# A four-layer graph kernel on one core: SAGE's gathered rows taken apart into a float32r leading part and an exact rest

## The chip, the core and the metric

The kernel runs on one core of a Trainium2 chip (trn2). Times are microseconds of device time of that core. The time before the change is 3072.85 us, the median of three runs (3069.26 to 3073.18). One more execution was profiled; it took 3070.05 us, and its span, from the first to the last instruction, is 3067.8 us.

## The reference

The model has 3327 nodes with 512 features, padded to 3328 = 26 blocks of 128, and a sparse 0/1 adjacency matrix. Each of four layers normalizes the rows, takes the positive part, runs a graph layer and adds its result to the rows. Layers 0, 2 and 3 are attention layers. Layer 1, which the change touches, is GraphSAGE:

```python
mask = (adj > 0).astype(x.dtype)
deg = jnp.sum(mask, axis=1, keepdims=True)
agg = mask @ x / jnp.maximum(deg, 1.0)
self_f = x @ W_self + b_self
nb_f = agg @ W_nb + b_nb
combined = jnp.concatenate([self_f, nb_f], axis=-1)
out = combined @ W_comb + b_comb
return jax.nn.relu(out)
```

Everything is float32. `mask @ x` is what the changed lines compute: for each node the sum of its neighbours' rows.

## The kernel before, in words

**Lists.** The kernel doesn't multiply by the whole mask. The nodes that receive are cut into 52 groups of 64 (`GB`), two to a block of 128 (`PG` = 2, counted by `u`). For each group a first stage lists the nodes that any of its 64 members has as a neighbour, in *chunks* of 128. How many chunks a group may have stands in `CAPS`: 22, 15, 13, 12, 11, 10, 9 and so on down to 5 and 4, in all 359. A chunk's 128 rows are fetched with one indirect DMA (`gather`, issued on GpSimd's queue at L995); a mask of 128 x 64 bytes (`mask`) says which of its rows belongs to which of the group's 64 nodes.

**Stages.** `sparse` runs attention layer 0 (`attend`), then the batch norm and layer norm of its result, then SAGE, then attention layers 2 and 3. While SAGE ends a block, `Following` (`proj`) already prepares the table of layer 2 from it: norm, transposes, three products, and two stores.

**SAGE.** The normalized rows are stored to `h_dram` (L1266). `own` multiplies each block by the weights for the node itself (`s_ps`, L1276) and adds the bias (L1277). Then come the *parts*: a part takes up to two chunks (`SUNIT`) of each of a block's two groups. For a part, `load` takes per group a tile `z_rows` (one of 8 buffers, `SROWS`), casts the byte mask to float32 with ScalarE into `z_mask` (L1333), and gathers the rows. The main loop asks for part i + 2 (`SAHEAD`) and then multiplies part i: one float32 matmul per chunk, mask as the stationary side (128 x 64), rows as the moving side (128 x 512), into the 64 partitions of `sage_acc` that belong to group `u` (L1352). The two groups of a block alternate, chunk by chunk.

When a block's sums are there, `ending` divides them by the degree on ScalarE (`s_ag`, L1291), transposes them with TensorE (`a_ps`, L1295), copies them (`aT`, L1297), multiplies by the neighbour weights (`n_ps`, L1301), and on VectorE adds the own part and the residual (`s_o`, L1306 and L1307). `Following.norm` and `rest` go on: three ScalarE passes over `s_o`, a few small VectorE operations (`rs_h`, `rs_g`, `rs_y`, L633 to L639), `ln_h` (L694), transposes (`p_ps`, L701), products (`p_sd`, L708 and L710; `p_wh`, L722), the small rows `v_row` and `r_row` (L713, L716, L719), and eight scalings of `p_wh` into `v_row` (L730). These steps are generators; `tick()`, called once per row of chunks, moves each by one step.

**What sets the order.** The attention layers' order is written out by hand. The SAGE stage isn't: a scheduler places its instructions on each engine's queue when the program is built, so that, for example, the matmuls of a part stand among those of `ending` and `Following`. Each engine then works through its own queue in order and waits at semaphores. A buffer is free for its next use when the last reader is done: a gather into `z_rows` waits for the matmuls of the part four parts earlier.

Of the kernel before, what the change touches and what calls it, by code (L numbers as in the profile page):

```python
# [22 lines left out]

F32 = mybir.dt.float32
BF16 = mybir.dt.bfloat16
I32 = mybir.dt.int32
I8 = mybir.dt.int8
U8 = mybir.dt.uint8
# [2 lines left out]
ALU = mybir.AluOpType  # L31
# [5 lines left out]
P = 128  # L37
H = 8
F = 64
D = H * F  # L40
# [8 lines left out]
GB = 64  # L49
CAPS = (22, 15, 13, 12, 11, 10, 9, 9, 9) + 4 * (8,) + 6 * (7,) + 11 * (6,) + 21 * (5,) + (4,)  # L50
# [5 lines left out]
UNIT = 3  # L56
SUNIT = 2
SROWS = 8
SAHEAD = 2
SMALL = 53.0  # L60
SHIFT = 20.0
# [4 lines left out]
def general(ctx: ExitStack, tc: tile.TileContext, t: dict, out: bass.AP):  # L66
# [22 lines left out]
    x3 = dram.tile([NP, D], F32, name="x3")  # L89
    bias_dram = dram.tile([NP, NP], BF16, name="bias_dram")  # L90
    recip_dram = dram.tile([1, NP], F32, name="recip_dram")
# [4 lines left out]
    nc.vector.memset(ones, 1.0)  # L96
    ones_bf = const.tile([P, P], BF16, name="ones_bf")
    nc.vector.memset(ones_bf, 1.0)
# [6 lines left out]
    with tc.tile_pool(name="setup", bufs=2) as sp, tc.tile_pool(name="setup1", bufs=1) as s1, tc.tile_pool(  # L105
# [4 lines left out]
        for c in range(NB):  # L110
            a = sp.tile([P, NP], I32, name="adjT_i", tag="adjT_i")
            nc.sync.dma_start(a, t["adjT"][c * P : (c + 1) * P, :])
            m = sp.tile([P, NP], BF16, name="mask_bf", tag="mask_bf")
            nc.vector.tensor_scalar(m, a, 0.0, None, ALU.is_gt)
# [7 lines left out]
        for b in range(nbk):  # L122
            w = min(BANK, NP - b * BANK)
            nc.vector.tensor_copy(deg[:, b * BANK : b * BANK + w], deg_ps[:, b, :w])
        alone = s1.tile([P, NP], BF16, name="alone")
        nc.vector.tensor_scalar(alone, deg, 0.0, -OFF, ALU.is_equal, ALU.mult)
# [25 lines left out]
    def gat(layer, xin, W, a_i, a_j, finish):  # L152

        with ExitStack() as lx:
# [58 lines left out]
            with tc.tile_pool(name=f"mx{layer}", bufs=2) as mp, tc.tile_pool(  # L213
# [3 lines left out]
                for q in range(NQ):  # L217
# [6 lines left out]
                    for c in range(NB):  # L224
                        mb = mp.tile([P, QW], BF16, name="mb", tag="mb", bufs=3)
                        if layer == 0:
                            a = mp.tile([P, QW], I32, name="adj_i", tag="adj_i", bufs=2)
                            nc.sync.dma_start(a, t["adj"][c * P : (c + 1) * P, q0 : q0 + QW])
# [4 lines left out]
                        for h in range(H):  # L233
                            junk = mp.tile([P, QW], BF16, name="junk", tag="junk", bufs=2)
                            nc.vector.tensor_tensor_reduce(
# [218 lines left out]
def products(ctx, tc, t):  # L454
# [5 lines left out]
    WA = pool.tile([P, 3, KC, 2 * H], F32, name="WA")  # L460
    ok = pool.tile([1, 1], I32, name="ok")
    with tc.tile_pool(name="wa1", bufs=1) as wp, tc.tile_pool(name="wa_ps", bufs=1, space=PSUM) as wps:
# [67 lines left out]
def constants(ctx, tc, N):  # L530
# [19 lines left out]
    c["pow"] = pw = const.tile([P, WB], F32, name="fpow")  # L550
    pi = const.tile([P, WB], I32, name="fpow_i")
    nc.gpsimd.iota(pi, pattern=[[-1, WB]], base=0, channel_multiplier=1)
# [10 lines left out]
class Projection:  # L563
# [4 lines left out]
    last, pb = "wh_ps", 1  # L568
# [10 lines left out]
    def block(self, c):  # L579
# [22 lines left out]
        for h in range(H):  # L602
            nc.scalar.mul(V[:, h, 0:F], wh[:, h * F : (h + 1) * F], V[:, h, F : F + 1])
        nc.sync.dma_start(self.table[c * P : (c + 1) * P, :ROW], row.bitcast(I32))

# [39 lines left out]
class Following:  # L645
# [29 lines left out]
    last = "p_ps"  # L675
# [291 lines left out]
def sparse(ctx: ExitStack, tc: tile.TileContext, t: dict, out: bass.AP, WA, ls, cs, idx, rdeg, first):  # L967
# [5 lines left out]
    nc = tc.nc  # L973
# [4 lines left out]
    PG = P // GB  # L978
# [13 lines left out]
    mask = keep.tile([P, NCH, GB], U8, name="mask")  # L992
# [167 lines left out]
    with ExitStack() as mx:  # L1160
# [64 lines left out]
        gp = mx.enter_context(tc.tile_pool(name="fsage", bufs=2))  # L1225
        gps = mx.enter_context(tc.tile_pool(name="fsage_ps", bufs=2, space=PSUM))
        two = [P, 2, D]
        with tc.tile_pool(name="fbn", bufs=1) as bp:
            var_ps = gps.tile([P, D], F32, name="var_ps", tag="n_ps")
            for c in range(0, NB, 2):  # L1230
# [3 lines left out]
                for i in range(2):  # L1234
                    k = used(c + i)
# [7 lines left out]
        with tc.tile_pool(name="fln", bufs=1) as bp:  # L1243
# [40 lines left out]
            for i in range(2):  # L1284
                own(NB - 2 + i)

        ends = []

        def ending(b, acc):
# [21 lines left out]
        def tick():  # L1311
            for e in list(ends):
                if next(e, 0) == 0:
                    ends.remove(e)
            proj.tick()


        parts = []
# [3 lines left out]
        loaded = {}  # L1322

        def load(i):
            if i >= len(parts):
                return
            zs = loaded[i] = []
            for u, kn in enumerate(parts[i][1]):
                if kn is not None:
                    k0, n = kn  # L1330
                    zt = gp.tile([P, SUNIT, D], F32, name="z_rows", tag="z_rows", bufs=SROWS)
                    mf = gp.tile([P, SUNIT, GB], F32, name="z_mask", tag="z_mask", bufs=SROWS)
                    nc.scalar.copy(mf[:, :n, :], mask[:, k0 : k0 + n, :])  # L1333
                    for k in range(n):
                        gather(zt[:, k, :], h_dram, k0 + k)
                        zs.append((k, u, k0 + k, mf[:, k, :], zt[:, k, :]))
            zs.sort(key=lambda x: x[:2])

        for i in range(SAHEAD):
            load(i)  # L1340
        for i, (b, _, begins, stops) in enumerate(parts):
            load(i + SAHEAD)
            if begins:
                acc = gps.tile([P, D], F32, name="sage_acc", tag="sage_acc")
            at = -1
            for r, u, k, m, z in loaded.pop(i):
                if r != at:
                    at = r
                    tick()
                g = b * PG + u  # L1350
                f, l = k == ls.first[g], k == ls.first[g] + CAPS[g] - 1
                nc.tensor.matmul(acc[u * GB : (u + 1) * GB, :], m, z, start=f, stop=l)  # L1352
            if stops:
                ends.append(ending(b, acc))
        while ends:
# [95 lines left out]
```

## Time and profile before

| what | value |
|---|---|
| time, median of 3 | 3072.85 us |
| profiled execution | 3070.05 us |
| its span | 3067.8 us |
| busy: PE, PEld, DVE, ACT, POOL | 2324.5, 1434.3, 1781.0, 1162.7, 1375.4 us |
| mean granted TensorE clock | 0.788 |
| first and last gather of `z_rows` | 1107.9 and 1704.6 us |
| first and last `s_ag` (block 0, block 25) | 1200.3 and 1727.8 us |
| `sage_acc` matmuls: records, busy | 718, 210.6 us |
| `z_rows` gathers: count, busy, mean | 359, 341.2 us, 950 ns |

How to read the profile: the engines are PE (TensorE), PEld (its weight loads, which overlap PE), DVE (VectorE), ACT (ScalarE), POOL (GpSimd) and SP. A row of a group names the line, the engine, the operation, out<-in by the program's names, shapes, how often; then busy us and mean ns, then the idle time just ahead of these instructions and what ended it. The matmuls' ends are modelled. In the timeline a row begins with the start and the duration in us; xN says how many equal instructions were merged, and brackets show idle time of the engine before it and what ended it. "issue" is time in which an engine waited for nothing that the profile shows. The page's chain of work that ended last is followed back from the last instruction. A few per cent of the matmul records can be missing.

### The profile page before, as it was taken

What the parts mean: (1) busy time and instruction counts of PE and PEld (TensorE: products, weight loads), DVE (VectorE), ACT (ScalarE), POOL (GpSimd) and SP (SyncE); (2) the same over time, 40 slices, a digit from 0 to 9 for tenths busy, and PEclk for the clock granted to TensorE, in tenths of its full rate; (3) what the DMA queues carried; (4) which work ended last, traced back from release to release, by engine and by line L of the source; (5) the groups of instructions that cost most, each with busy time, mean ns of one, the idle gap of its engine ahead of it and who ended that gap; (6) DMA issues with size and microseconds to landing.
All of it is one profiled execution on the core that took longest, in us unless ns stands there. A gap on an engine that the chain in (4) does not pass through costs nothing.

```text
span 3067.8 us, 55727 instructions
## 1 busy us (share of the span) xinstructions
PE 2324.5 (76%) x22046; PEld 1434.3 (47%) x22046; DVE 1781.0 (58%) x2077; ACT 1162.7 (38%) x4117; POOL 1375.4 (45%) x1462
## 2 busy tenths in 40 slices
PE   2888157877777797788888857888998857778876
PEld 1555034555554342333333345555665445555654
DVE  7434867787786840000111077777766457887886
ACT  3775012233334321344444402444666601222343
POOL 0000055566553026666554266555444155665653
PEclk9888678886777898889999867887877766675666
DMA  7671067777664455666666366566655256666774
GB/s 284 242 266 58 11 221 236 218 242 210 201 196 145 168 178 172 192 205 218 192 194 185 105 177 190 177 184 193 183 172 175 72 170 185 187 196 194 200 198 131
DMA packets 186641, 561.55 MB, mean 183 GB/s; under 512 B 35386, under 2 KB 40322, under 8 KB 183045
## 3 DMA queue, kind: packets, MB, share of 16 engines
q0 software_dynamic: 114880, 404.47, 45.2%
q1 hardware_dynamic: 70918, 153.04, 14.2%
q8 instruction: 177, 2.90, 0.4%
q14 instruction: 92, 0.75, 0.1%
q10 hardware_dynamic: 574, 0.39, 0.0%
HBM read 498.42 MB, written 59.36 MB: 182 GB/s over the span
## 4 chain that ended last, share of the span: by engine, by line
PE 63%; issue 13%; ACT 5%; DVE 2%; another core or an unknown queue 2%; DMA 1%; POOL 0%; DVEq 0%; SPq 0%; ACTq 0%; POOLq 0%
PE facc L1117 30%; PE p_wh L722 7%; PE r_bc L1028 6%; PE sage_acc L1352 5%; PE n_ps L1301 3%; PE p_sd L710 2%; PE p_sd L708 2%; PE s_ps L1276 2%; PE fwx_ps L1194 1%; PE bmean_ps L1204 1%; PE p_ps L701 1%; ACT v_row L730 1%; PE a_ps L1295 1%; DMA fWc<-in_L_gnn_W_comb 1%
## 5 line engine op out<-in xcount | busy, mean ns | idle before, releaser
L995 POOL DMA_INDIRECT rows<-table,idx x1077 | 1027.7, 954 | 1222.8 <-PE facc L1117 350.9
L1117 PE MATMUL facc<-rows,wgt 128*64 128x65 f32 x17232 | 958.0, 270 | 371.5 <-issue 358.0
L1117 PEld LDWEIGHTS facc<-rows,wgt 128*64 128x64 f32 x17232 | 820.8, 179 | 668.7 <-issue 588.7
L1103 DVE TENSOR_TENSOR wgt<-mx,mask 128x1536 f32<-128x1536 f32 (+1 forms) x405 | 638.4, 1576 | 168.2 <-PE facc L1117 78.6
L1096 DVE TENSOR_TENSOR mx<-r_bc,rows 128x1536 f32<-128x1536 f32 (+1 forms) x405 | 639.5, 1579 | 161.1 <-PE facc L1117 68.4
L995 POOL DMA_INDIRECT z_rows<-h_dram,idx x359 | 341.2, 950 | 395.2 <-ACT hT L1273 138.8
L1055 ACT ACTIVATE fhp<-sums,rd 64x64 f32<-64x64 f32 x832 | 219.7, 334 | 145.5 <-DVE rd L1049 71.3
L1028 PE MATMUL r_bc<-r_one,fones 1*128 1x512 f32 x312 | 217.8, 783 | 16.6 <-DMA r_one<-r_dram 8.6
L1352 PE MATMUL sage_acc<-z_rows,z_mask 128*64 128x512 f32 x718 | 210.6, 641 | 14.0 <-issue 7.7
L722 PE MATMUL p_wh<-fWt,hT 128*128 128x512 f32 x416 | 214.5, 661 | 2.0 <-ACT r_row L716 1.8
L1088 ACT ACTIVATE mask<-on 128x192 uint8<-128x192 uint16 (+1 forms) x135 | 46.5, 344 | 445.4 <-DVE on L1082 181.8
L1045 ACT COPY sums<-facc 128x260 f32<-128x260 f32 x156 | 57.5, 369 | 407.6 <-PE facc L1117 289.3
L719 DVE TENSOR_SCALAR r_row<-r_row 8x128 f32<-8x128 f32 x52 | 11.7, 226 | 307.3 <-ACT r_row L716 224.0
L1306 DVE TENSOR_TENSOR s_o<-n_ps,bn_y 128x512 f32<-128x512 f32 x26 | 17.9, 688 | 206.9 <-PE n_ps L1301 190.3
L722 PEld LDWEIGHTS p_wh<-fWt,hT 128*128 128x128 f32 x416 | 84.6, 215 | 107.1 <-issue 101.3
L589 PE MATMUL wh_ps<-fWt,hT 128*128 128x512 f32 x208 | 121.3, 709 | 2.8 <-ACT hT L776 2.8
L730 ACT ACTIVATE v_row<-p_wh,v_row 128x64 f32<-128x64 f32 x416 | 89.7, 321 | 73.8 <-PE p_wh L722 72.5
L1055 ACT ACTIVATE bn_y<-sums,rd 64x64 f32<-64x64 f32 x416 | 109.5, 333 | 2.4 <-DVE rd L1049 0.5
L1301 PE MATMUL n_ps<-fWx,aT 128*128 128x512 f32 x208 | 106.1, 649 | 5.1 <-ACT aT L1297 4.9
L1352 PEld LDWEIGHTS sage_acc<-z_rows,z_mask 128*64 128x64 f32 x718 | 51.7, 142 | 119.9 <-issue 105.6
L1276 PE MATMUL s_ps<-fWx,hT 128*128 128x512 f32 x208 | 96.1, 616 | 9.0 <-ACT hT L1273 9.0
L713 ACT ACTIVATE v_row<-p_sd 128x8 f32<-128x8 f32 x52 | 9.6, 184 | 240.5 <-PE p_sd L710 107.3
(196 smaller groups left out, 2291.3 us busy)
## 6 DMA issues: line engine op xcount, KB each, us to landing
adj_i<-in_adj SPq DMA_DIRECT2D x26, 1664.0 KB
table<-v_row SPq DMA_DIRECT2D x78, 264.0 KB
rows<-table,idx POOLq DMA_INDIRECT x1077
fin_x<-fx SPq DMA_DIRECT2D x52, 256.0 KB
ln_x<-in_x SPq DMA_DIRECT2D x26, 256.0 KB
bn_x<-in_x SPq DMA_DIRECT2D x13, 512.0 KB
fx<-bn_x SPq DMA_DIRECT2D x13, 512.0 KB
fsage_x<-fx SPq DMA_DIRECT2D x26, 256.0 KB
```

What stands on the lines that cost most here:

```text
L589: nc.tensor.matmul(wh, hT[:, kc, :], self.Wt[:, kc, :], start=(kc == 0), stop=(kc == KC - 1))
L722: nc.tensor.matmul(wh, hT[:, kc, :], self.Wt[:, kc, :], start=(kc == 0), stop=(kc == KC - 1))
L730: nc.scalar.mul(V[:, h, 0:F], wh[:, h * F : (h + 1) * F], V[:, h, F : F + 1])
L995: nc.gpsimd.indirect_dma_start(out=dst, out_offset=None, in_=src[:, :], in_offset=bass.IndirectOffsetOnAxis(ap=idx[:, k : k + 1], axis=0))
L1028: nc.tensor.matmul(rb, ones[0:1, :], rrs.pop(g), start=True, stop=True)
L1055: nc.scalar.mul(hp[o0 : o0 + GB, h * F : (h + 1) * F], sm[mine, q, 0:F], rd[mine, q, :])
L1096: nc.vector.tensor_tensor(mx[:, :n], rbs[g].unsqueeze(1).to_broadcast(full), gt[:, :n, H * (F + 1) : ROW].unsqueeze(3).to_broadcast(full), ...
L1103: nc.vector.tensor_tensor(wt[:, :n], mx[:, :n], mk.unsqueeze(2).to_broadcast(full), ALU.mult)
L1117: nc.tensor.matmul(accs[g][v * GB : (v + 1) * GB, q * (F + 1) : (q + 1) * (F + 1)], wt[:, k, h, :], gt[:, k, h * (F + 1) : (h + 1) * (F + 1)],
L1276: nc.tensor.matmul(ps, hT[:, kc, :], Wx[:, 0, kc, :], start=(kc == 0), stop=(kc == KC - 1))
L1301: nc.tensor.matmul(ps, aT[:, kc, :], Wx[:, 1, kc, :], start=(kc == 0), stop=(kc == KC - 1))
L1352: nc.tensor.matmul(acc[u * GB : (u + 1) * GB, :], m, z, start=f, stop=l)
```

## The change

In the SAGE stage, each gathered row tile is taken apart on VectorE: `z_high` is the row rounded to float32r, and what is left over replaces the row itself, in place. The masks are now float32r as well, and as wide as the block: 128 columns, of which the 64 of the other group stay zero, in eight tiles that are cleared once. Each chunk becomes two float32r matmuls, of the high and of the low part, into all 128 partitions of `sage_acc`; both groups of a block sum into the same accumulation, with one start and one stop per block. `halves(i + 1)`, the splitting of the next part, is asked for ahead of the matmuls of part i. `z_high` has four buffers (`SHALF`), `z_rows` still eight. The changed lines, with the imports and constants:

```diff
+F32R = mybir.dt.float32r
+SHALF = 4
@@ SAGE
+        hp = mx.enter_context(tc.tile_pool(name="fhalf", bufs=1))
...
                     zt = gp.tile([P, SUNIT, D], F32, name="z_rows", tag="z_rows", bufs=SROWS)
-                    mf = gp.tile([P, SUNIT, GB], F32, name="z_mask", tag="z_mask", bufs=SROWS)
-                    nc.scalar.copy(mf[:, :n, :], mask[:, k0 : k0 + n, :])
+                    mf = wide[u][i % len(wide[u])]
+                    nc.scalar.copy(mf[:, :n, u * GB : (u + 1) * GB], mask[:, k0 : k0 + n, :])
                     for k in range(n):
                         gather(zt[:, k, :], h_dram, k0 + k)
-                        zs.append((k, u, k0 + k, mf[:, k, :], zt[:, k, :]))
-            zs.sort(key=lambda x: x[:2])
+                    zs.append((u, k0, n, mf, zt))
+
+        def halves(i):
+            if i >= len(parts):
+                return
+            zs = []
+            for u, k0, n, mf, zt in loaded.pop(i):
+                zh = hp.tile([P, SUNIT, D], F32R, name="z_high", tag="z_high", bufs=SHALF)
+                nc.vector.tensor_copy(zh[:, :n, :], zt[:, :n, :])
+                zl = zt.bitcast(F32R)
+                nc.vector.tensor_tensor(zl[:, :n, :], zt[:, :n, :], zh[:, :n, :].bitcast(F32), ALU.subtract)
+                zs += [(k, u, k0 + k, mf[:, k, :], zh[:, k, :], zl[:, k, :]) for k in range(n)]
+            split[i] = sorted(zs, key=lambda x: x[:2])
+
+        split = {}
+
+        wide = []
+        for u in range(PG):
+            wide.append([])
+            for i in range(SAHEAD + 2):
+                mf = gp.tile([P, SUNIT, P], F32R, name=f"z_mask{u}{i}", bufs=1)
+                nc.vector.memset(mf.bitcast(F32), 0.0)
+                wide[u].append(mf)
         for i in range(SAHEAD):
             load(i)
+        halves(0)
         for i, (b, _, begins, stops) in enumerate(parts):
             load(i + SAHEAD)
+            halves(i + 1)
             if begins:
                 acc = gps.tile([P, D], F32, name="sage_acc", tag="sage_acc")
-            at = -1
-            for r, u, k, m, z in loaded.pop(i):
-                if r != at:
-                    at = r
-                    tick()
-                g = b * PG + u
-                f, l = k == ls.first[g], k == ls.first[g] + CAPS[g] - 1
-                nc.tensor.matmul(acc[u * GB : (u + 1) * GB, :], m, z, start=f, stop=l)
+            zs = split.pop(i)
+            for r in sorted({z[0] for z in zs}):
+                tick()
+                for half in (4, 5):
+                    for z in zs:
+                        if z[0] == r:
+                            last = stops and half == 5 and z is zs[-1]
+                            nc.tensor.matmul(acc, z[3], z[half], start=begins, stop=last)
+                            begins = False
             if stops:
                 ends.append(ending(b, acc))
```

## The prediction

> **What bounds the kernel now.** I read the page first, then the windows of the SAGE stage, the timeline, the waits and the chain inside those windows, and last the built order of both programs. Only the SAGE stage changes: the gathers from `h_dram` run from 1108 to 1705 us, its last `s_ag` is at 1727.8. I split it at 1160 (the last `own`) and at 1447 (the `s_ag` of block 10; the 26 blocks count from 0). The stretches below give us of busy time and (records) of PE, PEld, DVE, ACT, POOL, then granted clock, DMA share, GB/s; a second answer gives the same for `sage_acc` alone.
>
> ```profile
> 1108.00:1160.00 52.00, 46.36 (x132) 20.47 (x132) 6.92 (x10) 5.22 (x13) 20.69 (x22) 0.93 0.38 112
> 1160.00:1447.00 287.00, 223.23 (x764) 86.28 (x760) 20.96 (x57) 93.87 (x389) 182.67 (x192) 0.89 0.65 198
> 1447.00:1730.00 283.00, 248.16 (x923) 109.80 (x924) 33.25 (x92) 136.84 (x562) 137.74 (x146) 0.92 0.58 180
> ```
>
> ```profile
> 1160.00:1447.00 287.00, 116.93 (x392) 30.48 (x388) 7.15 (x11) 0.89 0.65 198
> 1447.00:1730.00 283.00, 88.16 (x308) 19.97 (x308) 11.08 (x16) 0.92 0.58 180
> ```
>
> The late stretch (15 blocks of 9 to 12 chunks, a chunk being one gather of 128 rows) is TensorE's: 248 of 283 us. In the heavy stretch a gather costs POOL 0.95 us and 0.30 us of issue, so 192 x 1.25 = 240 of 287 us: POOL and PE (223) share the bound. DVE has next to nothing to do. In the chain, `sage_acc` has 27.7% of the heavy stretch and 22.3% of the late one.
>
> The timeline of PE says what a chunk costs now:
>
> ```profile
> 1512.34 1.07 PE L1352 MATMUL sage_acc<-z_rows,z_mask 128*64 128x512 f32 x2
> 1519.17 3.60 PE L722 MATMUL p_wh<-fWt,hT 128*128 128x512 f32 x8
> 1522.70 3.65 PE L1352 MATMUL sage_acc<-z_rows,z_mask 128*64 128x512 f32 x16
> 1526.87 1.08 PE L1352 MATMUL sage_acc<-z_rows,z_mask 128*64 128x512 f32 x4
> ```
>
> An f32 matmul is two records. A full-width one takes 0.43 us a record (x8 in 3.60), 0.86 a matmul. A chunk alone takes 1.07, but two chunks (x4) also 1.08, and eight (x16) 3.65: a pair for groups u=0 and u=1, which write the two halves of PSUM's partitions, runs side by side.
>
> **What the Trainium skill says.** "FP8 and Floating Point Precision", TensorE Precision Notes: true FP32 is four passes of the array, the reduced form a truncation to some 22 bits. Four passes in 0.86 us fit; a pass of 512 columns is then 0.215 us (estimate); no f32r runs here yet. "TensorEngine Tiling (Array Packing)", When to Use Tiling: a stationary side of 64 columns or fewer allows two column tiles at once. The x2 and x4 rows agree. "VectorE: DVE Perf Modes", the perf-mode tier table: an fp32 copy in SBUF reaches 2x, `tensor_tensor` stays at 1x. `L897` and `L853` below agree. "SBUF — State Buffer", SBUF: two separate sides: while DVE runs a 2-port op (an fp32 copy is one), GpSimd can't write a gather's descriptors until that op ends. The trace shows it even for an op with two SBUF inputs:
>
> ```profile
> 1237.59 0.94 POOL L995 DMA_INDIRECT z_rows<-h_dram,idx  x1 [0.30 <-issue]
> 1237.96 0.69 DVE L1306 TENSOR_TENSOR s_o<-n_ps,bn_y 128x512 f32<-128x512 f32 x1 [11.36 <-PE n_ps L1301]
> 1238.68 0.69 DVE L1307 SCALAR_TENSOR_TENSOR s_o<-s_o,fsage_x 128x512 f32<-128x512 f32 x1
> 1238.84 1.35 POOL L995 DMA_INDIRECT z_rows<-h_dram,idx  x1 [0.30 <-issue]
> ```
>
> The gather that starts inside L1307 ends 0.82 us after it and takes 1.35 instead of 0.94. One that is under way when L1306 starts (an input in PSUM) takes 0.94. A DVE op already started isn't lengthened.
>
> **The change, part by part.**
>
> *Matmuls.* 359 chunks were 718 records; they become 718 f32r matmuls (each row of gathers: high, low) of 128 columns, all into the whole of PSUM's partitions, so nothing is paired. At one pass: 718 x 0.215 = 154 us against 210.6 busy (116.9 + 88.2 + 5.5). But a pair goes from 4 x 0.215 = 0.86 side by side to 4 x 0.215 in a row: nothing is won there. What is won is chunks alone: the timeline has 26 lone x2 groups, each 1.07 to some 0.58 (two passes and the same 0.15 of start): 13 us; the rest of the 57 us is half-clock time after stalls, which stays. I take -10 us of path; bounds -35 (all of it counts where PE is the bound) to +50 (f32r needs two passes, or its weight loads don't hide; the `p_sd` rows, x8 in 0.95 us, put a weight load at 0.12 us at most, under a pass of 0.215).
>
> *DVE splits.* Per group and part one copy and one subtraction; the mask casts count 163 of two rows and 33 of one. Prices:
>
> ```profile
> L853 DVE TENSOR_SCALAR adj_b<-adj_i 128x3328 bf16<-128x3328 int32 x26 | 49.0, 1885 | 8.4 <-DMA adj_i<-in_adj 6.4 <-PE words_ps L859 2.0
> L1232 DVE TENSOR_TENSOR bn_d<-bn_y,bn_mean 128x1024 f32<-128x1024 f32 x13 | 15.8, 1225 | 14.0 <-PE var_ps L1236 8.5 <-ACT bn_d L1233 5.5
> L897 DVE TENSOR_SCALAR bit<-at 116x1664 int32<-116x1664 int32 x11 | 11.3, 1024 | 0.3
> ```
>
> L853 and L897 (one SBUF input, one with a cast) give (1885 - 1024) / 1664 = 0.52 ns an element: a copy of 1024 is 0.69 us, of 512 0.43; at 1x it would be 1.23, the upper bound. Subtractions: 1.23 (L1232) and 0.69. Sum: 163 x 1.92 + 33 x 1.12 = 350 us on an engine that was busy 54 of 570 us. A full part (4 chunks) is 4 x 0.06 of gaps + 3.83 = 4.07 us of DVE.
>
> *POOL against DVE.* With DVE busy 4.07 us of a part of about 6 (0.68), a gather starting at random waits 0.68 x the mean rest of an op (sum of squares 3.97 / 2 x 3.83 = 0.52) = 0.35 us. Cadence 1.60, times 192 = 307 us against 287: +20 in the heavy stretch. If gathers fall into step with the op ends, 1.3 us, 250 us, hidden: 0. Late: 10 x 1.6 = 16 of 18.6 us a block, hidden.
>
> *DVE's queue.* It is in order, and holds `s_o`, `r_row`, `rs_h`, `rs_g`, `rs_y` of the next layer's rows. Their waits were free:
>
> ```profile
> DVE r_row L719 <- ACT r_row L716: 185.9, 19, 21.0
> DVE s_o L1306 <- PE n_ps L1301: 181.3, 17, 48.4
> ```
>
> In the built order after, a late block's DVE queue is: six copies and six subtractions, then `s_o` to `rs_y`, then the next block's. From `s_o` to the end of `rs_y` the trace has 5.2 us (1607.45 to 1612.68) and, every second block, where ScalarE comes late, 10.5 us (1622.28 to 1632.78). The splits of ten chunks are 9.9 us and 12 gaps, 10.6. In a row: 15.8 and 21.1, mean 18.5 us. Now such blocks take 19.9 and 17.3 us between their `s_ag`s, mean 18.6. So DVE's row becomes as long as TensorE's cycle, no longer; two queues of one length that wait for each other lose something, of which I take +5 us for the 15 blocks. Behind the waiting `r_row` stand the copies, behind them TensorE's matmuls, behind those the buffers that POOL waits for (8, still). Bounds: 0 if ScalarE comes in time, +40 if all blocks take DVE's 21.1 (2.5 us in each of 15).
>
> *Start.* In the built order all `s_ps` now precede the first `sage_acc`; before, seven chunks ran among them and six more gathers (22 by 1160, against the 16 that eight buffers hold) were issued: 6 x 1.25 = 7.5 us, I take +5; bounds 0 and +8. Memsets of eight masks: in DVE's free 3 us between `bn_d`s, 0; the same number of mask casts, 0.
>
> Sum: -10 + 20 + 5 + 5 = +20 us. Profiled execution: 3067.8 of span, 3070.05 in all, so 3090; the shown median is 2.8 above it: 3093.
>
> **Rivals.** *DVE hides everything, faster: this is the one on the other side.* DVE stood idle nine tenths of the stage, PE is the largest share of the chain. Late sage work falls from 88 to 154 chunks x 0.43 = 66 us, -22; heavy -10: 3073 - 32 = 3041. Against it: the DVE row of 18.5 us a late block. It comes about if ScalarE is no longer late in every second block. *f32r not in one pass:* a matmul of 0.43 us makes 309 us of them; late PE is 248 / 15 = 16.5 us a block now and 16.5 + (132 - 88) / 15 = 19.5 then, at today's share of 0.88 22.1 against 18.7, +51; with heavy +40 (of 200 x (0.86 - 0.58) = 56 and POOL's 20 together) 3073 + 91 = 3164. A loss that I count as small becomes a plain one from some 0.3 us a matmul on. Against: the skill's four passes. *GpSimd shut out* of the 0.06 us gaps between splits, so gathers and splits alternate: 4.07 + 5.0 = 9.1 us a part in place of 6, 192 x 2.27 = 436 against 287, +149: 3222 or more. It decides once a gather loses two gaps in a row. Nothing in the trace shows two such ops in a row with a gather waiting. *No change:* gains and losses cancel, within 6 us.
>
> **How the numbers follow.** My forecast 0.43 (own range 3079 to 3130), faster 0.26, no change 0.14, two passes 0.10, GpSimd shut out 0.07. A measurement tells about 0.2%, 6 us. Faster 0.26, same 0.14, slower 0.43 + 0.10 + 0.07 = 0.60. The range leaves out the shut-out case and the outer edges of faster and two passes: 3040 to 3160.
>
> **What would show it.** Right: `sage_acc` busy near 160 to 175 us at some 0.22 us a matmul; DVE 350 us more; z_rows gathers with a mean of 1.2 to 1.4 us; `z_high` copies behind waits for ACT `r_row`; the last `s_ag` at 1740 to 1760. Wrong: gathers still 0.95 us; late blocks 16 to 17 us apart (faster); 0.43 us per f32r matmul (two passes); gathers of 2 us (shut out).

## The result, and the profile after

The changed kernel takes 3072.66 us (median of 12 runs), the kernel before beside it 3073.86 us (12 runs): ratio 1.0003, 95% interval 0.9986 to 1.002. That is no change that can be measured; 20 us more were forecast. The profiled execution of the changed kernel has a span of 3077.7 us, 9.9 more than that of before; 8.7 of them lie ahead of the first gather of the SAGE stage, in work that is the same in both.

One thing has to be said before any number is compared: every kernel of this case ran in one of two kinds of session. In some, to which the times above belong, the kernel before takes 3025 to 3081 us (**B sessions** below), in others 2615 to 2633 us (**A sessions**). The forecast was made from a trace of a B session. All ratios are taken within one session. The expectations quoted below speak of "kinds of chips"; but the same chip number showed both kinds, so what differs is not known to be the chip.

The stage in the three stretches of the prediction, cut at the same events: *start* from the first gather to the `s_ag` of block 0, *heavy* to that of block 10, *late* to that of block 25.

| profiled execution, us | start | heavy | late | stage |
|---|---|---|---|---|
| before, on record | 92.4 | 246.4 | 281.1 | 619.9 |
| changed, on record | 102.7 | 262.8 | 255.8 | 621.3 |

So the change moves much: +10, +16 and -25 us. The same windows as shown for before, first of all instructions, then of `sage_acc` alone (us of busy time and records of PE, PEld, DVE, ACT, POOL; then clock, DMA share, GB/s):

```profile
1116.60:1219.00 102.40, 72.45 (x187) 36.90 (x185) 41.77 (x51) 9.63 (x27) 55.04 (x43) 0.83 0.37 107
1219.00:1482.00 263.00, 212.63 (x704) 127.47 (x703) 168.61 (x233) 93.58 (x376) 205.48 (x170) 0.86 0.64 197
1482.00:1738.00 256.00, 237.48 (x917) 146.90 (x916) 171.70 (x269) 136.00 (x552) 179.53 (x148) 0.95 0.65 198
```

```profile
1116.60:1219.00 102.40, 32.03 (x75) 18.01 (x75) 0.00 (x0) 0.83 0.37 107
1219.00:1482.00 263.00, 119.51 (x332) 68.79 (x331) 6.90 (x10) 0.86 0.64 197
1482.00:1738.00 256.00, 96.41 (x313) 59.52 (x312) 10.84 (x16) 0.95 0.65 198
```

The busy time of `sage_acc` has not fallen: it is 248 us in all, 210.6 before. That column misleads here: it is made of the modelled lengths of single matmuls, for an f32r matmul 0.4 us or more (0.475 on average). What a matmul costs in the row is read from the starts. The timeline of PE:

```profile
1587.58 0.63 PE L1381 MATMUL sage_acc<-z_rows,z_mask 128*128 128x512 f32 x2
1588.05 0.62 PE L1381 MATMUL sage_acc<-z_high,z_mask 128*128 128x512 f32 x2
1588.51 0.62 PE L1381 MATMUL sage_acc<-z_rows,z_mask 128*128 128x512 f32 x2
1588.97 0.62 PE L1381 MATMUL sage_acc<-z_high,z_mask 128*128 128x512 f32 x2
```

Two matmuls every 0.465 us: 0.23 each, one pass. In the stretches where the granted clock is 0.5, most start 0.43 apart. The groups on the page:

```profile
L998 POOL DMA_INDIRECT z_rows<-h_dram,idx x359 | 440.1, 1226 | 307.3 <-ACT hT L1276 140.6
...
L1353 DVE TENSOR_TENSOR z_rows<-z_rows,z_high 128x1024 fp32r<-128x1024 f32 (+1 forms) x196 | 214.0, 1124 | 0.3
...
L1351 DVE CAST z_high<-z_rows 128x1024 fp32r<-128x1024 f32 (+1 forms) x196 | 126.3, 662 | 124.6 <-DMA z_rows<-h_dram,idx 82.4
```

The splits cost 214.0 + 126.3 = 340 us of DVE. A gather has gone from 0.95 to 1.226 us. In the heavy stretch POOL has 205.48 us of gathers and 170 x 0.30 of issue, 256 of 263 us: **GpSimd is its bound now**. And the waits of DVE in the late stretch, where `r_row` had waited for ScalarE before:

```profile
DVE rs_h L636 <- ACT ln_j L688: 20.9, 10, 2.5
DVE z_high L1351 <- DMA z_rows<-h_dram,idx: 13.5, 7, 4.8
DVE s_o L1310 <- PE n_ps L1305: 10.3, 5, 3.5
...
DVE r_row L722 <- issue: 3.6, 1, 3.6
```

Of the waits for `r_row`, 66.4 us behind ScalarE in the late stretch of before, 5 us are left. Where it came from is seen in a block of the late stretch of before, in the timeline:

```profile
1622.97 1.04 PE L710 MATMUL p_sd<-hT,WA 128*8 128x128 f32 x8
...
1624.95 3.70 PE L722 MATMUL p_wh<-fWt,hT 128*128 128x512 f32 x8
...
1629.41 0.19 ACT L713 ACTIVATE v_row<-p_sd 128x8 f32<-128x8 f32 x1 [10.19 <-PE p_wh L722]
...
1629.90 0.28 DVE L719 TENSOR_SCALAR r_row<-r_row 8x128 f32<-8x128 f32 x1 [6.20 <-ACT r_row L716]
```

and in one of the changed kernel:

```profile
1602.47 1.04 PE L713 MATMUL p_sd<-hT,WA 128*8 128x128 f32 x8
...
1603.55 0.18 ACT L716 ACTIVATE v_row<-p_sd 128x8 f32<-128x8 f32 x1 [5.13 <-PE p_sd L713]
```

`v_row` needs `p_sd`. In before, ScalarE stood idle for 5.4 us after the recorded end of `p_sd` (1624.01) until it could start; in the changed kernel 0.04 us. (The ends of matmul records are modelled, but `p_wh`, behind it in the queue, has its start at 1624.95.) I call this a **late hand-over**: TensorE's result reaches the others later than its records say. Counted for this one place (from the recorded end of `p_sd` to `v_row`, as far as ScalarE was idle, for the 24 that come before the last `s_ag`): before has 17 of 24 later than 1 us, 93.7 us in all, 41.1 of them in the late stretch; the changed kernel 3, 9.6 and 1.4.

Two other explanations can be looked for in the trace of before. `v_row` might have waited for the store of an older `v_row` tile; but in all 17 cases the semaphore that TensorE steps, and that `v_row` waits for, makes its last step 0.02 us before `v_row` starts (here it stands still from 1622.26 to 1629.38). TensorE might have run at half clock, more slowly than its records show; but in only 3 of the 17 cases does the granted clock fall below 1.0 between the recorded end of `p_sd` and `v_row` (here it is 1.0 from 1604.2 to 1634.9). So it is TensorE's signal that comes late, and in most cases not for a lower clock. Whether TensorE itself worked later than its records say isn't shown.

### The profile page after: what moved, and what is told of

It is laid out like the page before. It is cut to its first block, busy times and chain, and to the rows that moved or that the text cites. A ratio compares the mean times of both kernels' runs of the same rounds, so it can differ in the third digit from the quotient of the medians.

```text
span 3077.7 us, 56471 instructions
## 1 busy us (share of the span) xinstructions
PE 2330.7 (76%) x22046; PEld 1529.4 (50%) x22046; DVE 2103.2 (68%) x2477; ACT 1168.4 (38%) x4117; POOL 1472.8 (48%) x1462
## 4 chain that ended last, share of the span: by engine, by line
PE 58%; issue 16%; ACT 4%; DVE 4%; DMA 2%; POOL 1%; another core or an unknown queue 0%; DVEq 0%; SPq 0%; ACTq 0%; POOLq 0%
PE facc L1120 29%; PE r_bc L1031 6%; PE p_wh L725 6%; PE sage_acc L1381 4%; PE n_ps L1305 3%; PE p_sd L713 2%; PE p_sd L711 2%; DMA z_rows<-h_dram,idx 1%; PE fwx_ps L1197 1%; PE s_ps L1279 1%; PE bmean_ps L1207 1%; POOL z_rows L998 1%; PE p_ps L704 1%; DVE z_rows L1353 1%; ACT fhp L1058 1%
## 5 line engine op out<-in xcount | busy, mean ns | idle before, releaser
L1120 PE MATMUL facc<-rows,wgt 128*64 128x65 f32 x17232 | 946.6, 269 | 379.9 <-issue 351.5
L998 POOL DMA_INDIRECT z_rows<-h_dram,idx x359 | 440.1, 1226 | 307.3 <-ACT hT L1276 140.6
L1353 DVE TENSOR_TENSOR z_rows<-z_rows,z_high 128x1024 fp32r<-128x1024 f32 (+1 forms) x196 | 214.0, 1124 | 0.3
L1351 DVE CAST z_high<-z_rows 128x1024 fp32r<-128x1024 f32 (+1 forms) x196 | 126.3, 662 | 124.6 <-DMA z_rows<-h_dram,idx 82.4
L1381 PE MATMUL sage_acc<-z_high,z_mask 128*128 128x512 f32 x359 | 148.0, 479 | 49.6 <-DVE z_high L1351 30.1
L1381 PE MATMUL sage_acc<-z_rows,z_mask 128*128 128x512 f32 x359 | 148.5, 472 | 24.3 <-DVE z_rows L1353 16.9
L1381 PEld LDWEIGHTS sage_acc<-z_high,z_mask 128*128 128x128 f32 x359 | 74.5, 210 | 90.2 <-issue 54.9
L707 ACT ACTIVATE hT<-p_ps 128x128 f32<-128x128 f32 x208 | 55.6, 283 | 137.5 <-PE facc L1120 89.1
```

Source lines behind the costliest of these rows:

```text
L998: nc.gpsimd.indirect_dma_start(out=dst, out_offset=None, in_=src[:, :], in_offset=bass.IndirectOffsetOnAxis(ap=idx[:, k : k + 1], axis=0))
L1120: nc.tensor.matmul(accs[g][v * GB : (v + 1) * GB, q * (F + 1) : (q + 1) * (F + 1)], wt[:, k, h, :], gt[:, k, h * (F + 1) : (h + 1) * (F + 1)],
L1351: nc.vector.tensor_copy(zh[:, :n, :], zt[:, :n, :])
L1353: nc.vector.tensor_tensor(zl[:, :n, :], zt[:, :n, :], zh[:, :n, :].bitcast(F32), ALU.subtract)
L1381: nc.tensor.matmul(acc, z[3], z[half], start=begins, stop=last)
```

## The experiments

All stages, by the cuts above; the ratio is that of the times, to the kernel before in the same session, with its interval. Each row of stretches is one profiled execution. e1, e2 and e3 (A) and e7 (B) are the kernels of e9, e16, e10 and e13 once more. Two traces of one kernel differ in a stretch by up to 9 us in A (hybrid, late: 243.3 and 234.2) and 15 us in B (dead bn_stats, heavy: 278.5 and 293.4), so that smaller differences between two rows say little.

| kernel | session | start, heavy, late | stage | ratio of times |
|---|---|---|---|---|
| before (e11) | A | 66.4, 214.2, 230.1 | 510.7 | |
| changed (e12) | A | 94.9, 257.5, 240.5 | 592.8 | 1.0289 (1.0266 to 1.0312) |
| hybrid (e9) | A | 66.1, 224.0, 234.2 | 524.4 | 1.0077 (1.0053 to 1.0102) |
| no splits (e10) | A | 70.5, 212.9, 219.4 | 502.8 | 0.9975 (0.9963 to 0.9986) |
| dead splits (e16) | A | 80.8, 277.6, 262.4 | 620.8 | 1.0441 (1.0424 to 1.0457) |
| dead bn_stats (e17) | A | 75.6, 225.4, 252.3 | 553.3 | 1.0145 (1.0126 to 1.0165) |
| copy on ScalarE (e4) | A | 84.2, 255.0, 253.7 | 592.9 | 1.0306 (1.0278 to 1.0335) |
| full rest (e18) | A | 94.4, 254.8, 243.1 | 592.3 | 1.0294 (1.0274 to 1.0313) |
| before (e5) | B | 92.4, 245.3, 276.9 | 614.6 | |
| changed (e6) | B | 101.9, 254.7, 250.8 | 607.3 | 0.9994 (0.9979 to 1.0009) |
| hybrid (e15) | B | 91.1, 247.7, 248.7 | 587.5 | 0.9918 (0.9889 to 0.9948) |
| no splits (e14) | B | 97.9, 261.4, 270.5 | 629.8 | 1.003 (1.0013 to 1.0047) |
| dead bn_stats (e13) | B | 92.1, 293.4, 280.1 | 665.6 | 1.0168 (1.0138 to 1.0197) |
| high only (e8) | B | 82.3, 281.6, 236.6 | 600.6 | 0.9994 (0.9974 to 1.0015) |

### Hybrid: float32 early, float32r late

From the changed kernel; float32 matmuls read the same masks, 64 columns at a time:

```diff
+EXACT = 11
+            if parts[i][0] < EXACT:
+                for u, k0, n, mf, zt in loaded.pop(i):
+                    m = mf.bitcast(F32)[:, :, u * GB : (u + 1) * GB]
+                    zs += [(k, u, k0 + k, m[:, k, :], zt[:, k, :]) for k in range(n)]
+                split[i] = sorted(zs, key=lambda x: x[:2])
+                return
...
+                if b < EXACT:
+                    for z in zs:
+                        if z[0] == r:
+                            g = b * PG + z[1]
+                            f, l = z[2] == ls.first[g], z[2] == ls.first[g] + CAPS[g] - 1
+                            nc.tensor.matmul(acc[z[1] * GB : (z[1] + 1) * GB, :], z[3], z[4], start=f, stop=l)
+                    continue
```

What was expected of e1, hybrid:

> The changed kernel with blocks 0 to 10 multiplied in plain float32 as before (no split, two column halves, from the same wide masks) and only blocks 11 to 25 in float32r. Theory A (the change loses in the heavy blocks, by VectorE's splits holding GpSimd's gathers, and wins as much in the late ones, by a shorter TensorE row): heavy stretch as before (first gather to the s_ag of block 10: 339 us), late stretch as changed (15 blocks in 256 us), together 595 in place of 620 us: some 25 us faster, ratio 0.992 (3048). Rival B (the late gain is only the earlier loss made good, because gathers that were held run further ahead later): late stretch 275 to 281 us, ratio 0.998 to 1.000.

It was 1.0072 (1.0058 to 1.0086): slower, in a session in which the kernel before took 2624 us. Neither theory had that, and it showed that sessions differ. The copies of this run:

What was expected of e9, hybrid:

> The kernel with blocks 0 to 10 in float32 and 11 to 25 in split float32r, once more, since the chips differ: one runs the kernel before in 2624 us, others in 3040 to 3074, with TensorE's matmuls of the attention layers (facc) at a lower granted clock. Theory A' (late gain and early loss are separate, and the late gain exists where TensorE is the late bound): on a chip with 3040 to 3074 us before, start and heavy stretch as before (92 and 246 us), late 251 to 256: ratio 0.991 to 0.994. On the other kind again 1.007. Rival F (the schedule as a whole sets the time, and what one stretch gains another loses): within 6 us on the slower kind too.

What was expected of e15, hybrid:

> Blocks 0 to 10 in float32, 11 to 25 in split float32r, for the slower kind. There start and heavy 92 and 246 us as before, late 250: 20 to 27 us faster, ratio 0.991 to 0.994; if stops move from one stretch to another, within 6 us. On the faster kind again 1.007.

e9 fell in an A session: 1.0077; of these 19 us 13.7 lie in the stage, 9.8 of them in the heavy stretch, whose matmuls are float32 as before. Why is open. e15 fell in a B session: 3015 against 3040 us, ratio 0.9918, stretches 91, 248 and 249 us as theory A' said. There it beats the kernel before, and by comparison across sessions the changed kernel too (0.9994 in e6). Its hand-overs at `p_sd` are late in 8 of the first 9 blocks, which are float32 (57 us), and in none of the 15 late ones (0.8 us in all).

### The two kernels beside the experiments

What was expected of e5, before:

> The kernel before, unchanged, for a trace beside the experiments: on their chip it takes 2624 us, not 3073. All theories: the SAGE stage from the first gather to the last s_ag takes some 515 us there (535 of the hybrid less its 20 us of loss), gathers of 0.95 us.

What was expected of e6, changed:

> The changed kernel, unchanged, beside the experiments. Theory A: the hold of the gathers costs on any chip, while the late gain is TensorE's and shrinks where TensorE is granted a higher clock; the hybrid already shows +19 us there, of which the heavy blocks can only add: 20 to 60 us slower than before, ratio 1.008 to 1.023. If the change is neutral on every chip: 0.998 to 1.002.

What was expected of e11, before:

> The kernel before for a trace beside these. On a chip of the slower kind start, heavy and late stretch of 92, 246, 277 us as seen; on the faster kind start 66, heavy 225 (both as in the hybrid, whose early blocks are the same), late 220 to 228 us, that is some 15 us a block, TensorE at full clock.

What was expected of e12, changed:

> The changed kernel beside these. On a chip of the slower kind again 0.998 to 1.002. On the faster kind: late blocks 16.2 us apart as in the hybrid (VectorE's row of splits and waits, as the prediction summed it, is then the longer one), heavy stretch 240 to 255 us: 1.012 to 1.025.

e5 and e6 fell in a B session, not in the A session for which their numbers were given, and repeat the record: 0.9994, +10, +9 and -26 us by stretch. Theory A there, that the change costs on any chip, did not come true. e11 and e12 fell in an A session: there the change costs 2.9%, more than the 1.2 to 2.5% expected; the late blocks came 16.0 us apart (16.2 expected), and the heavy stretch, at 257.5 us, lay just above its range. The kernel before is the one that differs between the sessions: its stage takes 511 us in A and 615 to 620 in B, that of the changed kernel 593 and 607 to 621. Windows of before (e11), heavy and late:

```profile
1083.50:1297.70 214.20, 193.15 (x706) 76.21 (x708) 21.10 (x56) 92.70 (x373) 161.34 (x170) 0.97 0.80 242
1297.70:1527.80 230.10, 229.88 (x913) 100.65 (x910) 34.12 (x93) 134.88 (x554) 141.16 (x149) 1.00 0.74 224
```

and of the changed kernel (e12):

```profile
1104.40:1361.80 257.40, 211.03 (x703) 128.20 (x703) 168.16 (x232) 93.05 (x376) 204.98 (x167) 0.84 0.66 196
1361.80:1602.30 240.50, 231.67 (x917) 143.30 (x916) 171.43 (x269) 134.77 (x551) 179.11 (x151) 0.99 0.71 216
```

In e11 nothing is lost: the heavy stretch is POOL's (161.34 + 170 x 0.30 = 212 of 214 us), the late one PE's at full clock (229.88 of 230.10), and no hand-over of the 24 is later than 0.04 us. In e12 the heavy stretch is still POOL's: 204.98 + 167 x 0.30 = 255 of 257 us. All of its 43 us are longer gathers. In B the heavy stretch of before has room: it takes 246 us with 204 of gathers and issue, so that the longer gathers add 16 us instead of 43. That the late hand-overs of before make this room is likely, but not shown by a run.

### No splits

```diff
-                zh = hp.tile([P, SUNIT, D], F32R, name="z_high", tag="z_high", bufs=SHALF)
-                nc.vector.tensor_copy(zh[:, :n, :], zt[:, :n, :])
                 zl = zt.bitcast(F32R)
-                nc.vector.tensor_tensor(zl[:, :n, :], zt[:, :n, :], zh[:, :n, :].bitcast(F32), ALU.subtract)
-                zs += [(k, u, k0 + k, mf[:, k, :], zh[:, k, :], zl[:, k, :]) for k in range(n)]
+                zs += [(k, u, k0 + k, mf[:, k, :], zl[:, k, :], zl[:, k, :]) for k in range(n)]
```

What was expected of e3, no splits:

> The changed kernel without copy and subtraction: both float32r matmuls of a chunk read the gathered tile itself (so the sum is twice the rounded rows: the exact rest is left out). TensorE's, ScalarE's and GpSimd's work is that of the change, VectorE's that of before. Theory A: gathers at 0.95 us again, the heavy stretch at or below before's 339 us, the late one 250 to 256 us: 30 to 50 us faster than before, ratio 0.984 to 0.990. Rival D (the changed order of the queues makes the late gain and the heavy loss, not the prices of the operations): within 6 us of the changed kernel.

What was expected of e10, no splits:

> The changed kernel without copies and subtractions (the exact rest left out), once more for the same reason. Theory A': on a chip of the slower kind the heavy stretch at 240 us or below and the late one at 225 to 245 (nothing but TensorE's row is left: 14.4 us a block at full clock): ratio 0.980 to 0.988. On the other kind again 0.9966. Rival F: within 6 us.

What was expected of e14, no splits:

> The changed kernel without copies and subtractions (the exact rest left out), for the slower kind. There, if float32r work is itself less stopped (as the changed kernel's stage of 607 us against 593 on the faster kind suggests), start 70 to 75, heavy 213 to 225, late 220 to 235: a stage of 505 to 530 in place of 615, ratio 0.965 to 0.975. If the stops come with any TensorE work, heavy 235 to 250 and late 235 to 260: 0.98 to 0.99. On the faster kind again 0.9975.

e3 and e10 (A): 0.9966 and 0.9975, 7 to 9 us faster. Theory A had 30 to 50. This is the whole gain of float32r, without its costs: late 219.4 against 230.1, -10.7 us; heavy stays POOL's. e14 (B): 1.003, late 270.5, with 14 of 24 hand-overs late (87 us). So float32r alone neither shortens the late stretch in B by more than 6 to 11 us (before: 276.9 and 281.1) nor makes the hand-overs prompt; both of my branches for B were wrong. The heavy stretch of e14 in B:

```profile
1201.00:1462.50 261.50, 199.28 (x706) 127.48 (x706) 20.95 (x57) 91.24 (x377) 154.29 (x163) 0.83 0.63 190
```

It is as long as that of the changed kernel, with gathers of 0.95 us (154.29 / 163) and without splits. So the +16 us on record would not by themselves show the longer gathers to be the cause; that rests on POOL being full in the changed kernel (256 of 263 us), on A, and on the dead splits below.

### Dead splits, and dead work that holds nothing

Both are made from the kernel before; the float32 matmuls stay. Dead splits, asked for ahead of each part's matmuls:

```diff
+        def halves(i):
+            for n, zt in whole.pop(i, ()):
+                zh = hp.tile([P, SUNIT, D], F32R, name="z_high", tag="z_high", bufs=2)
+                nc.vector.tensor_copy(zh[:, :n, :], zt[:, :n, :])
+                zl = hp.tile([P, SUNIT, D], F32R, name="z_low", tag="z_low", bufs=1)
+                nc.vector.tensor_tensor(zl[:, :n, :], zt[:, :n, :], zh[:, :n, :].bitcast(F32), ALU.subtract)
```

and in their place:

```diff
+                for k in range(n + 1):
+                    zs = hp.tile([P, nc.vector.BN_STATS_DIM], F32, name="z_stats", tag="z_stats", bufs=2)
+                    nc.vector.bn_stats(zs, zt[:, k % n, :])
```

What was expected of e2, dead splits:

> The kernel before, with the same VectorE copies and subtractions as in the change, but into tiles that nothing reads; the matmuls stay float32 and wait for the gathers alone. Theory A (hold): gathers of the heavy stretch get a mean of 1.2 us, cadence 1.5, that stretch 15 to 25 us longer; late blocks as before or up to 10 us longer in all; 15 to 35 us slower, ratio 1.005 to 1.011. Rival C (the loss of the heavy stretch is the path landing, split, matmul with the same eight buffers, not the hold): no splits stand in the path of a matmul, so within 6 us of before.

What was expected of e7, dead bn_stats:

> The kernel before with dead VectorE work as in the run with dead splits, but of an operation with one input and a result of six numbers (bn_stats of 512 columns, 0.68 us, three for two rows, two for one: 377 us against 350). Theory A (it is the hold of the gathers by operations with two row tiles in SBUF, not VectorE being busy): gathers at 0.95 us, within 15 us of before. Rival E (VectorE's in-order queue, s_o and r_row among the dead work, makes the loss of the dead splits): as slow as the dead splits, ratio 1.03 to 1.05, with gathers of 0.95 us. If bn_stats holds gathers too, their mean goes to 1.2 us.

What was expected of e13, dead bn_stats:

> The kernel before with 377 us of dead bn_stats on VectorE, once more. On the faster kind (2622 us before): if the heavy loss is the hold, gathers stay at 0.95 us, the heavy stretch at 214 to 220 us, the ratio at 0.998 to 1.008; if it is VectorE's occupied queue, heavy 250 us or more and 1.02 to 1.05 as with the dead splits (277 us, 1.043). On the slower kind again 1.013 to 1.020.

What was expected of e16, dead splits:

> The kernel before with dead copies and subtractions on VectorE. On the faster kind again 1.043, heavy stretch bound by GpSimd (gather mean 1.3 us and 0.30 of issue). On the slower kind, where the kernel before isn't bound by GpSimd in the heavy stretch: heavy 265 to 290 us, late 265 to 285, ratio 1.01 to 1.02 if the hold is all; above 1.02 if VectorE's queue adds to it.

What was expected of e17, dead bn_stats:

> The kernel before with dead bn_stats, beside the dead splits. On the faster kind, if the hold is the cause: gathers 0.95 us, heavy 214 to 220 us, ratio 0.998 to 1.008; if VectorE's occupied queue is: heavy 250 us or more, ratio above 1.02. On the slower kind again 1.016 (heavy 278 to 293 us with gathers of 0.95 us), which would leave the queue as a cause of its own there.

The dead splits came out at 1.0433 (1.0419 to 1.0446, e2) and 1.0441 (e16), more than theory A's 1.011; e7 (B) at 1.0164 (1.0139 to 1.0188). e16 and e17 stood side by side in one A session. The heavy stretch in e16:

```profile
1094.40:1372.00 277.60, 225.83 (x708) 79.60 (x710) 170.38 (x239) 94.56 (x376) 225.54 (x171) 0.91 0.64 189
```

and in e17:

```profile
1091.00:1316.40 225.40, 200.92 (x681) 72.96 (x681) 165.39 (x304) 92.87 (x357) 160.88 (x170) 0.98 0.75 228
```

The DVE time is nearly the same (170 and 165 us). With copy and subtraction a gather takes 1.32 us (225.54 / 171) and the stretch 277.6; with bn_stats 0.95 and 225.4; without either 214.2. So of 63 us in the heavy stretch 52 come with the **hold** of the gathers (the gathers themselves take 65 us more) and 11 with DVE's occupied queue, as far as the bn_stats occupy it as the splits do. The ratio of e17, 1.0145, lies between its two branches. The matmuls don't wait for the dead splits, so rival C, the path through the splits, isn't needed for the loss. In the late stretch bn_stats alone cost 22 of the dead splits' 32 us: there the in-order queue (`s_o` and the small operations behind row work) is the larger part. In B the bn_stats cost 33 to 48 us in the heavy stretch (e7: 278.5, e13: 293.4, against 245.3 in e5) with gathers of 0.95 us: there the queue is a cause of its own, which I had not expected.

### Less DVE work, and other numbers

Copy on ScalarE; the leading part alone; a maximum in place of the subtraction:

```diff
-                nc.vector.tensor_copy(zh[:, :n, :], zt[:, :n, :])
+                nc.scalar.copy(zh[:, :n, :], zt[:, :n, :])
```

```diff
-                nc.vector.tensor_tensor(zl[:, :n, :], zt[:, :n, :], zh[:, :n, :].bitcast(F32), ALU.subtract)
+                zl = zh
...
-                for half in (4, 5):
+                for half in (4,):
```

```diff
-                nc.vector.tensor_tensor(zl[:, :n, :], zt[:, :n, :], zh[:, :n, :].bitcast(F32), ALU.subtract)
+                nc.vector.tensor_tensor(zl[:, :n, :], zt[:, :n, :], zh[:, :n, :].bitcast(F32), ALU.max)
```

What was expected of e4, copy on ScalarE:

> The changed kernel with the copy into z_high on ScalarE; VectorE keeps the subtraction. Theory A: VectorE's holding time falls by a third (126 of 340 us), gathers to a mean of 1.1 us, heavy stretch 5 to 10 us shorter than changed; the late one pays with ScalarE (copies of 1.06 us as of bn_d, 10 chunks a block: 5 to 6 us of ScalarE's own 8.6 us a block), 0 to 30 us longer. In all -10 to +25 us against the changed kernel. If the hold didn't matter, the heavy stretch would stay at 365 us from the first gather to the s_ag of block 10.

What was expected of e8, high only:

> The changed kernel with the leading part alone: copy and one float32r matmul per chunk (the exact rest is left out). VectorE loses 214 us of subtractions, TensorE 359 matmuls of 0.23 us = 83 us. Theory A: the hold falls to the copies' 126 us, gathers to a mean of 1.05 us; the stage gets shorter than that of the kernel before, ratio to before 0.975 to 0.995. Against the run without splits (0.9966) it tells the copy's hold from TensorE's work: if TensorE sets the late end, late blocks fall from its 14.6 us by half of 20 x 0.23 = 2.3 us.

What was expected of e18, full rest:

> The changed kernel with a maximum in place of the subtraction: the same instructions and waits, but the second matmul multiplies a full rounded row, not a small rest (so the sum is twice the rounded rows). On the slower kind: late stretch 249 to 256 us and the ratio to before at 0.998 to 1.002 if the pace of the splits is what spares TensorE its stops; late 265 to 275 us and a ratio of 1.004 to 1.008 if it is the small numbers. On the faster kind as the changed kernel, 1.029, in both cases.

e4 (A): gathers fall to a mean of 1.117 us, as said, but the heavy stretch by 2.5 us only (255.0 against 257.5) and the late one grows by 13: the stage is that of the changed kernel. e8 (B): half the matmuls and a third of the splits, and still 0.9994. Its gathers take 0.992 us (1.05 expected), against 1.117 with the subtractions alone in e4: of the two operations of a split the subtraction holds more. Its late stretch is 14 us shorter than the changed kernel's (e6), its heavy one 27 us longer. What is saved in one stretch was lost in another; not what theory A said. 12 of 23 hand-overs are late (50 us), but 10 of them (38 us) in the late stretch, which is the shortest of all in B; the hand-overs don't account for the 27 us, whose cause is open. e18 fell in an A session and equals the changed kernel, as said for that kind; the question that it was made for, in B, was not answered.

## Why the prediction was wrong, step by step

- **Matmuls, -10: right.** One pass, 0.23 us (0.215 was the estimate). Where TensorE alone is the bound (no splits, A, late) the gain is 10.7 us. Pairs gain nothing: eight paired chunks took 3.65 us before, and sixteen matmuls at 0.23 take 3.7. A chunk alone took 1.07, and two f32r matmuls 0.63 to 0.72.
- **Splits, 350 us: right,** 340.
- **POOL against DVE, cadence 1.60, +20 in the heavy stretch: about right.** Cadence 1.51 (256 us for 170 gathers), +16 on record, +9 in e6. (The prediction's stretch began at 1160 and so held part of the start.) The whole price, where POOL is the bound before too, is +43 (A).
- **GpSimd shut out:** wrong as a steady state, right in a run of splits. At the start, DVE went through the splits of eight tiles from 1165.90 to 1179.88 with no gap over 0.1 us (first and last row shown), and a gather issued at 1171.15 waited for the last. POOL's and then DVE's timeline:

```profile
1171.15 9.55 POOL L998 DMA_INDIRECT z_rows<-h_dram,idx  x1 [34.87 <-PE sage_acc L1381]
1181.00 0.95 POOL L998 DMA_INDIRECT z_rows<-h_dram,idx  x1 [0.30 <-issue]
```

```profile
1165.90 1.28 DVE L1351 CAST z_high<-z_rows 128x1024 fp32r<-128x1024 f32 x2
...
1177.53 2.35 DVE L1353 TENSOR_TENSOR z_rows<-z_rows,z_high 128x1024 fp32r<-128x1024 f32 x2
```

It ends 0.82 us after DVE (1180.70 against 1179.88), as the one in the prediction did. The gaps between these operations let no gather in. Later DVE mostly waits for data after two to four operations, and the mean stays at 1.226. The Trainium skill ("SBUF — State Buffer", SBUF: two separate sides) calls the pair of ports that VectorE and GpSimd share an exclusive lock held for the whole instruction; in this trace a gather waited for some ten instructions in a row.
- **Start, +5, bounds 0 and +8: right in kind, too small.** +10.3 on record. As forecast, `sage_acc` now begins behind the last `own` (at 1166.7 us; in before at 1115.5, among them): GpSimd waits 34.9 us for it, and then comes the gather of 9.55 us. In A, where before has a start of 66.4 us, it is +28.5.
- **DVE's queue, a late block of 15.8 and 21.1 us in turn, +5: this is the step that failed.** The late stretch came out at -25. The 21.1 rested on "every second block, where ScalarE comes late". ScalarE wasn't late by itself. It waited 5.4 us for `p_sd` in every second block from 1592 to 1704 us (21.1 less 5.4 is 15.7): late hand-overs, which the A sessions don't have at all and which, in the late stretch of the changed kernel, are all but gone (1.4 us in all for 41.1). I took a wait that belonged to one kernel's run for a constant of the stage. With punctual hand-overs I had 15.8 for each block; in e12 the late `s_ag`s are 240.5 / 15 = 16.0 us apart on average, the last ten 14.0 to 15.4. DVE is busy 171.43 / 15 = 11.4 us a block there. So the 15.8 was somewhat too long and no bound of these blocks. The rival "DVE hides everything" named the condition (ScalarE no longer late in every second block), but it was wrong in its size for the matmuls (22 for 11), put the heavy stretch at -10 (+16 measured) and left out the start.

That gains and losses cancel within 6 us was among the rivals ("No change"), but it named no terms. The sum on record: +10.3 + 16.4 - 25.3 = +1.4 us of stage. Three of the signs named for a right forecast came (gathers of 1.226 us, 340 us more of DVE, 0.23 us a matmul); the sign against it came too, late blocks of about 17 us (255.8 / 15). It is not that the change does nothing; in A sessions, without late hand-overs to win back, it is 1.0289.

**Open:** what makes TensorE's results come late in B, and why blocks with splits are spared. float32r alone doesn't do it (e14), DVE work beside float32 only in part (e13: 11 of 24 late by over 1 us, 31.9 us in all), copies with half the matmuls don't either (e8). Copies, subtractions and f32r together go with prompt hand-overs, in e6, in the late blocks of e15 and on record. Whether it is the pace of the splits or the small numbers of the rest was not tried in B. That the late hand-overs cost before its 25 us is argued from 41.1 us of them against 1.4, from e15 and from A; no run takes them away alone.

## What to carry to other kernels

Before a wait is put into a forecast as a fixed cost, look whether its releaser had long ended by its own record: such a wait belongs to the conditions of that run, and may leave with the change. In a kernel that gathers through GpSimd, price VectorE's copies and subtractions of row tiles by what they add to each gather (here 0.28 us, 43 us in the stretch where GpSimd is the bound), not by VectorE's idle share. And a ratio near 1 may be two large terms: split the stage at fixed events, and try the change where each term acts alone (the hybrid: 0.9918 where the change as a whole gave 0.9994).

## What was not expected of the hardware

- The same program takes 2622 or 3040 us by session, and the effect of a change has another sign in them: hybrid 1.0077 and 0.9918, changed kernel 1.0289 and 0.9994. A sessions: no hand-over at `p_sd` later than 0.04 us in any of the eleven traces. B sessions: up to 17 of 24 later than 1 us (before), by up to 13.2 us (e15).
- bn_stats of 512 columns (0.68 us, one input, six numbers out) left gathers at 0.95 us, where a copy and a subtraction of the same rows in SBUF made them 1.32; that it still cost 33 to 48 us of the heavy stretch in B, and 11 in A, was not expected.
- Half clock goes with the waits: most f32r matmuls start 0.43 us apart where the granted clock is 0.5, and 0.23 where it is 1.0. The Trainium skill ("TensorE: Matmul & The Clock Gate", Part 1: The HAM clock gate) says that the array's clock is halved after idle time. This agrees: in before, late, the mean granted clock is 0.92 in B, with its late hand-overs, and 1.00 in A, without them.
